# Graph attention prologue: where value stores are issued, when later weights are turned, and in which order attention takes its memory

## The chip, the cores and the metric

The kernel runs on one core of one Trainium2 chip. Its time is the device time in microseconds (us) of one launch; of several runs the median is given. A core has five engines that work side by side, each through its own list of instructions in order: TensorE (PE: matrix products and transposes into PSUM), VectorE (DVE), ScalarE (ACT), GpSimd (POOL) and SyncE (SP), which only issues DMAs. ACT and POOL can issue DMAs too; what an engine issues stands in its own list, between its other work. An engine that waits holds back all that stands behind in its list.

## The reference, cut to what matters

`x` has 3327 rows (N) of 128 features (D), `adj` is 3327 x 3327. There are four layers, each followed by a layer norm over the features:

```
# layer 0, H = 8; Wq, Wk, Wv: 1024 x 128
q = (x @ Wq.T).reshape(128, 3327, 8)      # the flat buffer read anew: d, n, h
k = (x @ Wk.T).reshape(128, 3327, 8)
v = (x @ Wv.T).reshape(128, 3327, 8)
a = einsum('dnh,dmh->dnm', q, k) * 128 ** -0.5 + adj + adj
out = einsum('dnm,dmh->dnh', softmax(a), v).reshape(3327, 1024)
x = layernorm(x + out @ Wo.T)
# layers 1 to 3: products of adj or adj.T with x and small weights
x = layernorm(x + a_norm @ (x @ W1.T + b1))
x = layernorm(x + (adj/deg) @ x @ W_in + (adj.T/deg_T) @ x @ W_out)
x = layernorm(x + x @ W_self.T + (adj @ x) @ W_neigh.T + b3)
```

The attention has 128 "heads" d, each with 3327 queries and keys of length 8. Its exponentials, 128 x 3327 x 3327 of them, are the bulk of the work.

## The kernel before, in words

There are three stages.

**Prologue** (lines 248 to 409). The tokens are taken in seven blocks u of 512 (NU = 7, the last is half full). For each block `split` (342) forms the query products, then the key products: up to four tiles of 128 x 1024 in PSUM (`products`, L292), each copied by ACT into a rounded part `hi` (L348), with the remainder `lo` formed by DVE (L349). POOL issues the stores of both to the DRAM images `q_s` and `k_s` (`store_slots`, L286). DVE also takes the block's largest `hi` (L351, `top_q`, `top_k`). `values_projected` (306) forms the values (L311), copied to `vp` by DVE and ACT in turn (`copy`, L144 and L146). `values_turned` (315) then brings the values into the layout that attention reads: some 42 small products a block (L330) into PSUM, copied to `vo` (again L144/L146). Whenever sixteen d are turned, four stores of `vo` to the image `v_img` go out, issued from ACT (L339), 1.66 MB together. In blocks 1 to 4 a row block of `adj` is loaded (`ar`, L370) and its row maxima taken by DVE (L371); in block 4 (`store_tops`, L219) they are split into `rhi` and `rlo`, and POOL issues their stores to `lead_s` (L228), element by element. `vo` and `ar` share two buffers (tag "wide"), `hi` and `lo` have two each, so a new one waits until the store or the use of the one before the last is over.

After the loop the weights of the later layers are loaded, transposed on PE and stored to DRAM (lines 376 to 388: `w1T`, `w3T`, and the eight pieces of `woT`; the stores are issued from POOL). Then `flag` is formed: a bound on the scores from `top_q` and `top_k`, taken over all partitions with `partition_all_reduce` on POOL (L394), then three small operations of DVE. It decides after attention whether a slow, safe version is to be run. Last, constants are stored to `klead_s` and `k_s` (402 to 409).

The order of the prologue isn't the order of the text: a scheduler places each engine's instructions by their dependences. So some of the text's last parts run early.

**Attention** (412 to 706). 7 column blocks of 476 queries x 4 key ranges make 28 blocks b; in each, 32 groups g of four d. For each d PE forms scores (L625) on top of the transposed `adj` (`e_in`, L618), ACT takes the exponentials (L633; a part runs on DVE), and PE weighs the values with them (L651). The order is written out by hand for PE, ACT, POOL and DVE (`manual_schedule`). Loads are issued from SP: `load_edges` (432, L442, one part per 128 queries, four in all, the last with 92 rows), `load_heads` (460) with queries `qt` (L479), keys `kt` (L486), constant rows of the keys (L492) and, for the first group of a column block, rows from `lead_s` into `qt` (L501), and `load_values` (518, L522). `copy_queries` (506) completes `qt` on DVE (L510 to L512). Memory for these tiles comes from pools that are entered one after the other: accumulators `acc` and value pads (`accp`), `kq` (`kt`, `qt`, `vs`), `ed` (`e_in`), `ex` (exponentials), `pe2`. They take over the memory that the prologue's pools leave, in that order, so a tile's first write waits for the last use of what lay there. `prepare` (557) is called ahead of each d.

DMAs issued from SP and ACT share eight completion semaphores in turn; a DMA that gets one waits until the DMA eight places earlier has landed.

**Later layers** (from line 1000): products with `adj` and its transpose.

Of the kernel before, what the change touches and what calls it, by code (L numbers as in the profile page):

```python
# [10 lines left out]
F32 = mybir.dt.float32  # L11
# [3 lines left out]
ALU = mybir.AluOpType  # L15
AX = mybir.AxisListType
# [3 lines left out]
P = 128  # L20
GROUP = 4
# [15 lines left out]
QK_SAFE = 20.0  # L37
# [13 lines left out]
def kernel(ctx: ExitStack, tc: tile.TileContext, x, adj, wq, wk, wv, wo,  # L51
# [14 lines left out]
    nc = tc.nc  # L66
# [67 lines left out]
    rowsum = const.tile([P, T], F32, name="rowsum")  # L134
    colsum = const.tile([P, T], F32, name="colsum")
    flag = const.tile([P, 1], I32, name="flag")


    rsum = const.tile([P, NU, 4], F32, name="rsum")
# [108 lines left out]
    with tc.tile_pool(name="pw", bufs=1) as pw, tc.tile_pool(name="pa", bufs=2) as pa, \  # L248
# [43 lines left out]
                nc.tensor.matmul(pp[:, c:c + 512], lhsT=xT[:, u, r, :], rhs=w[:, c:c + 512], start=True, stop=True)  # L292
            return pp.rearrange("p (h j) -> p h j", h=H)

        top_q = pw.tile([P, NU], F32, name="top_q")
        top_k = pw.tile([P, NU], F32, name="top_k")

# [15 lines left out]
        def values_turned(d):  # L315

            g, i = d // 16, d % 16
            if i == 0:
                vo[g] = pa.tile([P, 4, T, 32], F32, tag="wide", name="vo")
            ps = pps.tile([P, 2, H, T], F32, tag="ps", bufs=3, name="vtr")  # L320
            for k in range(2):
                q, r = (d + k) * N // D, (d + k) * N % D
                for wrap in range(2 if r else 1):
                    at = q + wrap
                    while at < q + wrap + T:
                        u = at // SUPER
                        n = min(q + wrap + T, (u + 1) * SUPER) - at
                        s = at - q - wrap
                        first = (0 if wrap else P) + r
                        nc.tensor.matmul(ps[:, k, :, s:s + n], lhsT=turn[:, first:first + P],  # L330
                                         rhs=vp[u][:, :, at - u * SUPER:at - u * SUPER + n],
                                         start=(k == 0 and wrap == 0 and s == 0), stop=True,
                                         skip_group_check=True)
                        at += n
            copy(d // 2, vo[g][:, i // 4, :, i % 4 * H:(i % 4 + 2) * H].rearrange("p s (k h) -> p k h s", k=2), ps)
            if i == 14:
                for k0, nt in KBS:
                    w = nt * 32
                    nc.scalar.dma_start(out=flat_ap(v_img, k0 * HD + g * 4 * w, [[T * HD, P], [w, 4], [1, w]]),  # L339
                                        in_=vo[g][:, :, k0:k0 + nt, :].rearrange("p g s c -> p g (s c)"))  # L340

        def split(u, w, s, top, f):
# [11 lines left out]
            store_slots(nc.gpsimd, s, H, u, lo.bitcast(F32))  # L354


        tops = pw.tile([P, 4], F32, name="tops")

        d = 0
        for u in range(NU):  # L360
            split(u, wqT, q_s, top_q, SCALE / 2)
            split(u, wkT, k_s, top_k, 1.0)
            values_projected(u)
            last = u * SUPER + spread(u)[1] * P
            while d < D and (d + 1) * N // D + T < last:
                values_turned(d)
                d += 2
            if 1 <= u <= 4:
                ar = pa.tile([P, NP], F32, tag="wide", name="ar")
                load_rows(nc.sync, ar[:, 0:N], adj, u - 1)  # L370
                nc.vector.tensor_reduce(tops[:, u - 1:u], ar[:, 0:N], AX.X, ALU.max)  # L371
            if u == 4:
                store_tops(pw, 0, tops, P)
        assert d == D

        w1T = load_transposed(pw, ppw, w1, "w1T")
        nc.gpsimd.dma_start(out=w1T_s, in_=w1T.rearrange("p a b -> p (a b)"))
        w3T = load_transposed(pw, ppw, w3, "w3T")
        nc.gpsimd.dma_start(out=w3T_s, in_=w3T.rearrange("p a b -> p (a b)"))

        wo_raw = pw.tile([P, HD], F32, tag="w_raw", name="wo_raw")
        nc.sync.dma_start(out=wo_raw, in_=wo)
        woT = pw.tile([P, HD], F32, name="woT")
        for h in range(H):
            ps = ppw.tile([P, P], F32, tag="w_ps", name="w_ps")
            nc.tensor.transpose(ps, wo_raw.rearrange("p (j h) -> p h j", h=H)[:, h, :], ident)
            copy(h, woT[:, h * D:(h + 1) * D], ps)
        nc.gpsimd.dma_start(out=woT_s, in_=woT)

        top = pw.tile([P, 2], F32, name="top")  # L390
        nc.vector.tensor_reduce(top[:, 0:1], top_q, AX.X, ALU.max)
        nc.vector.tensor_reduce(top[:, 1:2], top_k, AX.X, ALU.max)
        topall = pw.tile([P, 2], F32, name="topall")
        nc.gpsimd.partition_all_reduce(topall, top, P, bass.bass_isa.ReduceOp.max)  # L394
        bound = pw.tile([P, 1], F32, name="bound")
        nc.vector.tensor_tensor(bound, topall[:, 0:1], topall[:, 1:2], ALU.mult)

        nc.vector.tensor_scalar(bound, bound, QK_SAFE / H / 1.001, None, ALU.is_gt)
        nc.vector.tensor_copy(flag, bound)


        zero = pw.tile([4 * H, 512], F32, name="zero")
        nc.vector.memset(zero, 0.0)
        one = pw.tile([1, 512], F32, name="one")
        nc.vector.memset(one, 1.0)
        nc.sync.dma_start(out=klead_s, in_=zero)
        for row in (0, 1):
            nc.sync.dma_start(out=klead_s[row:row + 1, :], in_=one)
        nc.sync.dma_start(out=k_s[:, SLOTS:RS], in_=zero[0:2 * H, :])


    def attention():
        with tc.tile_pool(name="acc", bufs=1) as accp, tc.tile_pool(name="kq", bufs=3) as kq, \
                tc.tile_pool(name="ed", bufs=1) as ed, tc.tile_pool(name="ex", bufs=1) as ex, \
                tc.tile_pool(name="pe2", bufs=1) as pe, \
                tc.tile_pool(name="psc", bufs=1, space=PSUM) as psc:
            NG = (NHG + PACK - 1) // PACK
# [42 lines left out]
            def load_heads(b, g):  # L460

                c0, kb = blocks[b]
                k0, nt = KBS[kb]
                ns = [(nt + 1) // 2, nt // 2]
                kt = kq.tile([P, GROUP, 4 * P], F32R, name="kt")
                qt = kq.tile([P, GROUP, CW], F32R, name="qt")  # L470
                qf = qt.bitcast(F32)
                kf = kt.bitcast(F32)

                d = g * GROUP
                if kb:
                    for half in range(2):
                        nc.sync.dma_start(out=qf[64 * half:64 * half + 64].rearrange("p a c -> p (a c)"), in_=qimg[g])
                for row, a, n in ((0, 0, 2 * H), (1, H, H), (1 + 2 * H, 0, H)) if kb == 0 else ():
                    nc.sync.dma_start(out=qf[row:row + 2 * n - 1:2],  # L479
                                      in_=flat_ap(q_s, a * RS + c0 + d * N, [[RS, n], [N, GROUP], [1, CW]]))  # L480
                for back in range(2):
                    j = 1 if back and g == 0 else 0
                    for rg in range(2):
                        for u in range(2):
                            row = 64 * rg + 32 * back + u
                            nc.sync.dma_start(  # L486
                                out=kf[row:row + 31:2, j:, 0:ns[rg] * P],
                                in_=flat_ap(k_s, (d + j - back) * N + (k0 + (ns[0] if rg else 0)) * P,
                                            [[RS, 16], [N, GROUP - j], [1, ns[rg] * P]]))
                if g == 0:  # L490
                    for rg in range(2):
                        nc.sync.dma_start(out=kf[64 * rg + 32:64 * rg + 64, 0, 0:ns[rg] * P],  # L492
                                          in_=klead_s[:, 0:ns[rg] * P])
                if g == 0 and kb == 0:
                    nc.vector.memset(qf[32:64, 0], 0.0)
                    u = c0 // SUPER
                    cut = min(CW, (u + 1) * SUPER - c0)
                    for uu, a, n in ((u, 0, cut), (u + 1, cut, CW - cut)):
                        for row, part in ((0, 0), (16, 1), (1, 1), (17, 0)):
                            if n:  # L500
                                nc.sync.dma_start(  # L501
                                    out=qf[32 + row:33 + row, 0, a:a + n],
                                    in_=flat_ap(lead_s[uu], part * SUPER + c0 + a - uu * SUPER, [[SUPER, 1], [1, n]]))
                return kt, qt
# [169 lines left out]
                        in_=acc[32 * j:32 * j + nb * A1, f, :])  # L674


            queue, place = [], 0
            with tc.manual_schedule(engines={mybir.EngineType.PE, mybir.EngineType.Activation,
                                             mybir.EngineType.Pool, mybir.EngineType.DVE}):
                for j in range(len(subs)):  # L680
# [5 lines left out]
                values[groups[0]] = load_values(*groups[0])  # L686
                for b, d in steps:
                    prepare(b, d)
                    for si in range(len(SETS[KBS[blocks[b][1]][1]])):
                        vector_work(b)  # L690
                        exponents(b, d, si)
# [573 lines left out]
```

## Time and profile before

| What | us |
|---|---|
| median of 3 runs | 10760.09 |
| lowest and highest | 10756.05, 10763.08 |
| span of the profiled execution | 10769.0 |
| of it PE busy | 10578.8 |
| ACT busy | 9583.6 |
| DVE busy | 7959.0 |
| POOL busy | 1555.0 |
| first exponential of attention starts (L633) | 337.22 |
| first load of the later layers issued (L1013) | 10007.39 |

The profile is of one execution, whose only time is its span. Its times are counted from the start of that span. "Busy" leaves out the issuing of DMAs; the timeline shows it in rows with a "q" behind the engine (ACTq, SPq, POOLq). A row's bracket gives how long the engine stood idle before it and what ended that. A product on PE is listed as MATMUL, its weights' load as LDWEIGHTS (PEld), which runs beside the product before it.

### The profile page before, as it was taken

To read this page: it belongs to the slowest core of one execution; us is meant where nothing else is said; L and a number is where in the kernel's file an instruction comes from. 1 tells how busy PE (TensorE), PEld (TensorE's weight loads), DVE (VectorE), ACT (ScalarE), POOL (GpSimd) and SP (SyncE) were. 2 spreads that over 40 slices of the span, in tenths; PEclk is the share of its full clock that TensorE was granted. 3 is DMA by queue.
4 is the path that set the end of the run, shared out by engine and by line. 5 is a ranking of instruction groups with operands and counts; after the bars stand their busy time and mean duration, and the time that the engine had idled before them with its cause. 6 is when DMAs were issued, how large, how long until landed. Compare 5 with 4: busy or idle time off the path is not lost. (4 is left out here: it accounts for less than half of the span.)

```text
span 10769.0 us, 200811 instructions
## 1 busy us (share of the span) xinstructions
PE 10578.8 (98%) x76941; PEld 4110.9 (38%) x76941; DVE 7959.0 (74%) x8554; ACT 9583.6 (89%) x10447; POOL 1555.0 (14%) x2742
## 2 busy tenths in 40 slices
PE   8899999999999999999999999999999999999999
PEld 5333333333333333333333333333333333333779
DVE  6677788877788778887788777878777777777412
ACT  3799999999999999999999999999999999999400
POOL 0111122111221111211122111121111100001200
PEclk9999999999999999999999999999999999999999
DMA  7678897788976889768888688886888867888676
GB/s 250 187 183 189 205 212 183 178 194 199 211 191 168 199 203 209 192 170 193 198 209 200 156 192 189 198 195 171 194 194 201 195 162 178 181 188 197 220 281 246
DMA packets 1013555, 2116.45 MB, mean 197 GB/s; under 512 B 206760, under 2 KB 730730, under 8 KB 998772
## 3 DMA queue, kind: packets, MB, share of 16 engines
q1 hardware_dynamic: 915358, 1972.12, 75.8%
q0 software_dynamic: 79616, 116.88, 3.7%
q8 instruction: 623, 10.21, 0.4%
q10 hardware_dynamic: 17620, 14.49, 0.4%
q14 instruction: 338, 2.76, 0.1%
HBM read 1863.03 MB, written 239.54 MB: 195 GB/s over the span
## 5 line engine op out<-in xcount | busy, mean ns | idle before, releaser
L633 ACT ACTIVATE e<-sc 128x952 f32<-128x952 f32 (+1 forms) x9968 | 9361.2, 1085 | 322.8 <-PE sc L625 295.0
L651 PE MATMUL o<-e,v_pad 128*32 128x476 f32 (+1 forms) x46592 | 5650.9, 573 | 43.2 <-DVE acc L664 18.6
L625 PE MATMUL sc<-qt,kt 64*128 64x476 f32 x23296 | 4494.8, 440 | 55.8 <-ACT e L633 33.9
L625 PEld LDWEIGHTS sc<-qt,kt 64*128 64x128 f32 x23296 | 2184.3, 184 | 4439.7 <-ACT e L633 3736.3
L595 DVE SCALAR_TENSOR_TENSOR e<-e,ey 128x952 f32<-128x952 f32 x2352 | 2706.5, 1151 | 77.4
L589 DVE TENSOR_SCALAR ey<-sc 128x952 int32<-128x952 f32 x784 | 901.2, 1149 | 1426.5 <-PE sc L625 1389.1
L651 PEld LDWEIGHTS o<-e,v_pad 128*32 128x32 f32 (+1 forms) x46592 | 1035.8, 108 | 1914.8 <-issue 1893.1
L526 POOL COPY v_pad<-vs 128x192 f32<-128x192 f32 (+1 forms) x896 | 439.0, 516 | 8029.8 <-DMA vs<-v_img 6501.4
L595 DVE SCALAR_TENSOR_TENSOR e<-ey 128x952 f32<-128x952 f32 x784 | 903.0, 1152 | 27.2
L595 DVE SCALAR_TENSOR_TENSOR e<-e,et 128x952 f32<-128x952 f32 x784 | 901.5, 1150 | 22.2
L237 POOL DMA_DIRECT2D adjT_s<-at x1352 | 760.4, 570 | 141.5 <-DMA adjT_s<-at 99.2
L590 DVE TENSOR_SCALAR et<-ey 128x952 int32<-128x952 int32 x784 | 519.5, 663 | 26.9
L592 DVE TENSOR_SCALAR ey<-ey 128x952 int32<-128x952 int32 x784 | 518.9, 662 | 27.1
L1101 PE MATMUL bank<-y,eT 128*128 128x128 f32 (+1 forms) x4056 | 473.9, 276 | 0.4 <-DVE h L1223 0.4
L1101 PEld LDWEIGHTS bank<-y,eT 128*128 128x128 f32 (+1 forms) x4056 | 465.3, 192 | 5.7 <-DVE h L1223 0.6
L664 DVE TENSOR_TENSOR acc<-o,acc 128x476 f32<-128x476 f32 x231 | 150.3, 651 | 284.5 <-PE o L651 284.0
L510 DVE TENSOR_SCALAR qt<-qt 32x1428 fp32r<-32x1428 f32 x224 | 201.8, 901 | 93.3 <-DMA qt<-q_s 64.2
L1061 ACT ACTIVATE rstd<-mv,eps 128x1 f32<-128x1 f32 x104 | 30.4, 293 | 265.2 <-DVE mv L1059 265.2
L512 DVE CAST qt<-qt 64x1904 fp32r<-64x1904 f32 x224 | 259.9, 1160 | 7.6
L671 POOL DMA_DIRECT2D o_s<-acc x308 | 200.4, 655 | 35.3 <-DVE acc L664 21.2
L1204 PE MATMUL bank<-a,y 128*128 128x512 f32 (+2 forms) x364 | 145.5, 562 | 0.0
L348 ACT ACTIVATE hi<-pp 128x1024 fp32r<-128x1024 f32 x52 | 52.7, 1024 | 95.4 <-PE pp L292 78.2
(151 smaller groups left out, 2286.6 us busy)
## 6 DMA issues: line engine op xcount, KB each, us to landing
qt<-qimg SPq DMA_DIRECT2D x1344, 476.0 KB
kt<-k_s SPq DMA_DIRECT2D x5320, 96.0 KB
kt<-k_s SPq DMA_DIRECT2D x1764, 128.0 KB
eT<-adjT_s SPq DMA_DIRECT2D x78, 1664.0 KB
qimg<-qt SPq DMA_DIRECT2D x224, 476.0 KB
vs<-v_img SPq DMA_DIRECT2D x224, 224.0 KB
adjT_s<-at POOLq DMA_DIRECT2D x1352, 32.0 KB, 5.0
vs<-v_img SPq DMA_DIRECT2D x224, 192.0 KB
```

Source lines behind the costliest of these rows:

```text
L237: nc.gpsimd.dma_start(out=flat_ap(adjT_s, (t * P + 32 * q) * NP + c * PIECE, [[NP, 32], [P, ns], [1, P]]), in_=at[32 * i:32 * i + 32].rear ...
L510: return [(0.9, None, lambda: nc.vector.tensor_scalar(qt[32:64, 1:], qf[0:32, 0:GROUP - 1], -1.0, None, ALU.mult)), (0.4, None, lambda: nc ...
L512: (1.2, None, lambda: nc.vector.tensor_copy(qt[64:128], qf[0:64]))]
L526: nc.gpsimd.tensor_copy(vp[:, 32:32 + nt * GROUP * 32].rearrange("p (x c) -> p x c", c=32)[:, :, 0:H], vs.rearrange("p (x c) -> p x c", c=H))
L589: nc.vector.tensor_scalar(yi, x, -58 * math.log(2.0), 2 ** 24 / math.log(2.0), ALU.max, ALU.mult)
L590: vec.append((0.7, of, lambda: nc.vector.tensor_scalar(ti, yi, UPPER, EXPONENT, ALU.bitwise_and, ALU.bitwise_xor)))
L592: vec.append((0.7, of, lambda: nc.vector.tensor_scalar(yi, yi, LOWER, QUARTER, ALU.bitwise_and, ALU.bitwise_or)))
L595: vec.append((1.2, of, lambda i=i, a=a: nc.vector.scalar_tensor_tensor(e, e if i else y, a, t if i == len(POLY) - 1 else y, ALU.add, ALU.m ...
L625: nc.tensor.matmul(s[:, i, 0:CW], lhsT=kt[64 * rg:64 * rg + 64, k, pos * P:(pos + 1) * P], rhs=qt[64 * rg:64 * rg + 64, k, :], start=False ...
L633: nc.scalar.activation(e[:, 0:n, :], s[:, 0:n, 0:CW], AF.Exp, scale=2.0)
L651: nc.tensor.matmul(o[32 * j:32 * j + 32, 0:CW], lhsT=values[b, g][:m, c:c + 32], rhs=es[b, g * GROUP + j, r][:m, :], start=(r == 0 and u = ...
L1101: nc.tensor.matmul(ps[:n, 0:D], lhsT=e[:m, s, :n], rhs=y[:m, s, col:col + D], start=(s == 0), stop=(s == T - 1))
```

## The change

The value stores (`v_img`) are issued from SP and no longer from ACT. The later weights are loaded, turned and stored in the loop, behind the values of blocks 2, 3 and 4, and their stores are issued from SP. The constants' stores stand ahead of the loop. `flag` is formed in attention: its reductions are placed at d = 16 of the first block, the rest at d = 32. Attention enters its pools in the order `ed`, `kq`, `acc`, `ex`, `pe2`. The keys of the very first group (b = 0, g = 0) are loaded from ACT's queue.

```diff
@@ ahead of the prologue
+    top_q = const.tile([P, NU], F32, name="top_q")
+    top_k = const.tile([P, NU], F32, name="top_k")
+
+    def set_flag():
+        top = const.tile([P, 2], F32, name="top")
+        nc.vector.tensor_reduce(top[:, 0:1], top_q, AX.X, ALU.max)
+        nc.vector.tensor_reduce(top[:, 1:2], top_k, AX.X, ALU.max)
+        topall = const.tile([P, 2], F32, name="topall")
+        nc.gpsimd.partition_all_reduce(topall, top, P, bass.bass_isa.ReduceOp.max)
+        yield
+        bound = const.tile([P, 1], F32, name="bound")
+        nc.vector.tensor_tensor(bound, topall[:, 0:1], topall[:, 1:2], ALU.mult)
+        nc.vector.tensor_scalar(bound, bound, QK_SAFE / H / 1.001, None, ALU.is_gt)
+        nc.vector.tensor_copy(flag, bound)
+        yield
@@ values_turned
-                    nc.scalar.dma_start(out=flat_ap(v_img, k0 * HD + g * 4 * w, [[T * HD, P], [w, 4], [1, w]]),
+                    nc.sync.dma_start(out=flat_ap(v_img, k0 * HD + g * 4 * w, [[T * HD, P], [w, 4], [1, w]]),
@@ ahead of the loop over blocks
+        def later_weights(i):
+            if i < 2:
+                name, w, dram = (("w1T", w1, w1T_s), ("w3T", w3, w3T_s))[i]
+                wT = load_transposed(pw, ppw, w, name)
+                nc.sync.dma_start(out=dram, in_=wT.rearrange("p a b -> p (a b)"))
+                return
+            wo_raw = pw.tile([P, HD], F32, tag="w_raw", name="wo_raw")
+            nc.sync.dma_start(out=wo_raw, in_=wo)
+            woT = pw.tile([P, HD], F32, name="woT")
+            for h in range(H):
+                ps = ppw.tile([P, P], F32, tag="w_ps", name="w_ps")
+                nc.tensor.transpose(ps, wo_raw.rearrange("p (j h) -> p h j", h=H)[:, h, :], ident)
+                copy(h, woT[:, h * D:(h + 1) * D], ps)
+            nc.sync.dma_start(out=woT_s, in_=woT)
+
+        zero = pw.tile([4 * H, 512], F32, name="zero")
...
+        nc.sync.dma_start(out=k_s[:, SLOTS:RS], in_=zero[0:2 * H, :])
@@ in the loop
             values_projected(u)
+            if 2 <= u <= 4:
+                later_weights(u - 2)
@@ behind the loop: the same weights (stored from gpsimd), flag and constants
-        w1T = load_transposed(pw, ppw, w1, "w1T")
-        nc.gpsimd.dma_start(out=w1T_s, in_=w1T.rearrange("p a b -> p (a b)"))
...
-        nc.sync.dma_start(out=k_s[:, SLOTS:RS], in_=zero[0:2 * H, :])
@@ attention
-        with tc.tile_pool(name="acc", bufs=1) as accp, tc.tile_pool(name="kq", bufs=3) as kq, \
-                tc.tile_pool(name="ed", bufs=1) as ed, tc.tile_pool(name="ex", bufs=1) as ex, \
+        with tc.tile_pool(name="ed", bufs=1) as ed, tc.tile_pool(name="kq", bufs=3) as kq, \
+                tc.tile_pool(name="acc", bufs=1) as accp, tc.tile_pool(name="ex", bufs=1) as ex, \
@@ load_heads: both kinds of key loads
+                keys = nc.sync if b or g else nc.scalar
-                            nc.sync.dma_start(
+                            keys.dma_start(
                                 out=kf[row:row + 31:2, j:, 0:ns[rg] * P],
-                        nc.sync.dma_start(out=kf[64 * rg + 32:64 * rg + 64, 0, 0:ns[rg] * P],
+                        keys.dma_start(out=kf[64 * rg + 32:64 * rg + 64, 0, 0:ns[rg] * P],
@@ the loop of attention
+            flagged = set_flag()
                     prepare(b, d)
+                    if b == 0 and d in (4 * GROUP, 8 * GROUP):
+                        next(flagged)
```

More of the change, by code (lines that the diff above doesn't have):

```diff
@@ L293, in products @@
             return pp.rearrange("p (h j) -> p h j", h=H)
-        top_q = pw.tile([P, NU], F32, name="top_q")
-        top_k = pw.tile([P, NU], F32, name="top_k")
         turn = pw.tile([P, 3 * P], F32, name="turn")
@@ L354, in split @@
             store_slots(nc.gpsimd, s, H, u, lo.bitcast(F32))
-        tops = pw.tile([P, 4], F32, name="tops")
+        def later_weights(i):
[12 more added lines that the diff above has]
+            nc.sync.dma_start(out=woT_s, in_=woT)
+        tops = pw.tile([P, 4], F32, name="tops")
+        zero = pw.tile([4 * H, 512], F32, name="zero")
+        nc.vector.memset(zero, 0.0)
+        one = pw.tile([1, 512], F32, name="one")
+        nc.vector.memset(one, 1.0)
+        nc.sync.dma_start(out=klead_s, in_=zero)
+        for row in (0, 1):
+            nc.sync.dma_start(out=klead_s[row:row + 1, :], in_=one)
+        nc.sync.dma_start(out=k_s[:, SLOTS:RS], in_=zero[0:2 * H, :])
         d = 0
@@ L374 @@
         assert d == D
-        w1T = load_transposed(pw, ppw, w1, "w1T")
-        nc.gpsimd.dma_start(out=w1T_s, in_=w1T.rearrange("p a b -> p (a b)"))
[L378 to L408, printed above, removed]
-        nc.sync.dma_start(out=k_s[:, SLOTS:RS], in_=zero[0:2 * H, :])
     def attention():
-        with tc.tile_pool(name="acc", bufs=1) as accp, tc.tile_pool(name="kq", bufs=3) as kq, \
-                tc.tile_pool(name="ed", bufs=1) as ed, tc.tile_pool(name="ex", bufs=1) as ex, \
+        with tc.tile_pool(name="ed", bufs=1) as ed, tc.tile_pool(name="kq", bufs=3) as kq, \
+                tc.tile_pool(name="acc", bufs=1) as accp, tc.tile_pool(name="ex", bufs=1) as ex, \
                 tc.tile_pool(name="pe2", bufs=1) as pe, \
@@ L674, in store @@
                         in_=acc[32 * j:32 * j + nb * A1, f, :])
-            queue, place = [], 0
+            queue, place, flagged = [], 0, set_flag()
             with tc.manual_schedule(engines={mybir.EngineType.PE, mybir.EngineType.Activation,
```

## The prediction

> **What bounds the kernel now.** I began with the page's slices: TensorE and ScalarE are full from the second slice on, and only the first slice (269 us) has room.
>
> ```profile
> PE   8899999999999999999999999999999999999999
> ACT  3799999999999999999999999999999999999400
> ```
>
> The change touches only the prologue (0 to 337 us, when the first exponential starts) and, in attention, five small instructions of DVE and two of POOL. Comparing the two programs' instruction lists engine by engine, all instructions after the 490th on PE, the 148th on ACT, the 247th on DVE, the 67th on POOL and the 71st on SP are the same, in the same order. So the forecast is: how much earlier does the first exponential start? Next, the prologue in stretches of 20 us (columns: length, busy PE, PEld, DVE, ACT, POOL, granted clock, DMA share, GB/s):
>
> ```profile
> 160.00:180.00 20.00, 19.78 (x84) 14.78 (x83) 16.31 (x13) 6.35 (x7) 2.34 (x3) 0.96 0.84 305
> 200.00:220.00 20.00, 19.38 (x60) 11.48 (x61) 17.10 (x12) 5.95 (x7) 2.66 (x3) 0.85 0.61 228
> 220.00:240.00 20.00, 15.58 (x60) 12.86 (x59) 3.79 (x6) 4.32 (x6) 0.00 (x0) 0.83 0.78 266
> 280.00:300.00 20.00, 8.49 (x17) 4.30 (x17) 9.37 (x7) 5.33 (x9) 7.01 (x11) 0.74 1.02 371
> 300.00:320.00 20.00, 10.05 (x45) 9.29 (x45) 2.88 (x8) 2.98 (x5) 1.59 (x3) 0.79 0.75 227
> 320.00:340.00 20.00, 7.85 (x28) 5.13 (x29) 5.72 (x10) 1.80 (x2) 3.12 (x7) 0.50 0.56 173
> ```
>
> TensorE is nearly full until 280 us; the holes lie at 220 to 240 and above all after 280. The timeline of ScalarE says why in the first two places: its queue issues the value stores, and an issue can last long.
>
> ```profile
> 217.05 9.52 ACTq L339 DMA_DIRECT2D v_img<-vo  x4
> 272.40 13.78 ACTq L339 DMA_DIRECT2D v_img<-vo  x4
> 286.28 1.94 ACT L348 ACTIVATE hi<-pp 128x1024 fp32r<-128x1024 f32 x2 [14.01 <-issue]
> ```
>
> TensorE's waits from 95 to 337 us (total, times, longest) show what reaches it: 9.3 us of L311 and 4.4 us of L330 are these two issues.
>
> ```profile
> PE sc L618 <- DMA e_in<-in_adj_dram: 14.9, 4, 9.9
> PE pp L292 <- DVE lo L349: 10.9, 4, 3.9
> PE pv L311 <- ACT vp L144: 10.5, 3, 9.3
> PE vtr L330 <- ACT vo L144: 5.9, 2, 4.4
> ```
>
> The third hole is the junction to attention: the last turned copy ends at 310.6, the first exponential starts at 337.22, 26.6 us later.
>
> ```profile
> 317.70 1.65 SPq L442 DMA_DIRECT2D e_in<-in_adj_dram  x4
> 321.01 0.37 POOL L394 PARTITION_ALL_REDUCE topall<-top  x1 [6.08 <-DMA e_in<-in_adj_dram]
> 322.09 2.17 SPq L479 DMA_DIRECT2D qt<-q_s  x3
> 324.31 6.70 SPq L486 DMA_DIRECT2D kt<-k_s  x8
> 337.22 1.36 ACT L633 ACTIVATE e<-sc 128x1428 f32<-128x1428 f32 x1 [23.20 <-DMA qt<-q_s]
> ```
>
> **What the Trainium skill says.** "DMA: Bandwidth & Descriptors", section Issuing engines are not separate DMA queues: a store moved to another engine's queue runs on the same 16 DMA engines, and only the issue time is saved. The trace gives that time: eight groups of four stores held ScalarE 3.10, 4.41, 4.62, 6.59, 9.52, 3.07, 13.78 and 3.07, in sum 48.2 us. The same page, Specifications: below 512 B a transfer is a read-modify-write. The trace agrees strongly: the two lead stores (L228, elements of 4 B, 2 KB each) took 11.2 and 20.0 us to land, and the core's DMA fell to 20 GB/s in 260 to 265 and again in 275 to 280. "TensorE: Matmul & The Clock Gate", Part 1: an idle array falls to half clock and needs about 3.4 us of work to recover. Here too: after the 9.3 us hole the clock was 0.50, and eight k products took 6.09 us against 3.60 at 261. "GPSIMD Engine Reference", 1.1: some operations need a library loaded at run time; the 6.08 us idle before L394 fits that.
>
> **Part by part.** *Stores on SyncE.* ScalarE is rid of 48.2 us of issuing. TensorE felt 1.53 (at 182.9) + 4.42 (227.7) + 9.31 (288.5) = 15.3 of it. What is late next decides how much stays.
> - 1.53: nothing. The next wait (3.45 at 199.9) is for DVE, whose row maxima (L371, 3.62 us) wait for `ar`, which shares buffers with `vo` and is loaded after the value stores landed. These start when the copies are ready, on either queue: same time.
> - 4.42: kept at first. But six of the eight `wo` transposes now lie in that stretch with one PSUM buffer between them; four waits of some 0.6 (L386 waited 0.94 and 0.39 before) plus 0.27 each cost about 3. The new order also puts block 5's turning behind all its k products, which wait for DVE (reduction 4.41, then 3.62): in before, the two were interleaved. I take the start of block 6's q products as unchanged, 271 us.
> - 9.31: ScalarE takes block 6's q tiles at once, not at 286. Then late is `lo` of block 6's k: its buffer is free when block 5's `k_s` lo store has landed. In before that store (267.5, 23.7 to landing) landed at 291.2, just ahead of its use at 294.3. In after both lead stores come behind q lo instead of around it, and q lo is finished sooner, since the maxima stand behind it on DVE: leads at some 253 instead of 255.8 and 260.1, two holes of about 7 us to 268, then 4 MB at the 390 GB/s of 280 to 285, 10.8 us, with the value stores beside it: 279 to 291, and I take 283.
>
> From that `lo` to the last turned copy before: 294.3 to 310.6, 16.3. Now three value copies of DVE and not one stand behind it, +0.9: 17.2. So the last copy ends at 283 + 17.2 = 300.2.
>
> *Weights.* One w1 and two w3 transposes already ran amid the prologue, as did five of the eight of `wo`; only three stood at the end, after the last turning matmul. Their stores leave POOL (0.56, 0.57, 0.62) for SP: nothing. Nor do the constants of `klead_s` cost anything: in both built programs they are among SP's first six DMAs.
>
> *Flag.* The first `qt` load waited for it (SP: 2.6 us at L479). It costs attention two reductions and three small operations, 5 x 0.15 = 0.8 us of DVE (81% busy), and 6.4 us of POOL (14% busy). What hides it: a `v_pad` copy is made a group ahead (eleven exponentials of 1.085 us, about 12). Uncovered it would cost at most 6.4, once.
>
> *Pools and second queue.* `e_in` no longer waits for the last stores to land; the first goes out at the last turning matmul, the others behind the four stores (issue 3.1). Through one queue go 1.66 MB of stores and 1.67 MB of `e_in`, at 300 GB/s 11 us; the fourth `e_in` landed 10.5 after its group's issue before, so I put it at +12 from the last copy. Stores landed at +7 before; then `qt` (SP) and `kt` (ACT) start together. But a DMA waits for the one eight places earlier: `kt` 7 and 8 and both `klead` wait for lead loads, and those for the fourth `e_in`. Hence +12, lead 2, four issues 2.4, landing 2, and 2.1 from first matmul to exponential (335.15 to 337.22): 20.5 instead of 26.6. Bounds 17.5 and 24. ScalarE's ten issues come before its first exponential, so nothing waits behind them.
>
> Sum: first exponential at 300.2 + 20.5 = 320.7, against 337.2: 16.5 us less. In the profiled execution 10769.0 becomes 10752.5; its span is 8.9 above the median of the runs, so from the median: 10760.1 - 16.5 = **10743.6**.
>
> **Rivals.** A measurement of this kernel can tell about 0.2% from no change, 21.5 us. (a) *More*: store landed by 279, turning at full clock (9.2 becomes 7.7), junction 17.5, and the gaps of 0.99, 1.50 and 2.31 behind the first exponentials close with the earlier loads: 25 + 4.8 = 30 less, 10730. For it speaks that everything in attention follows the loads; against it that TensorE will again be cold after waiting for the store. (b) *The k store takes the stall's place whole*: landed at 291 as now, junction 24: 291.2 + 17.2 + 24 = 332.4, 4.8 less, 10755. The DMA share of 1.02 in 280 to 300 speaks for it. (c) *Slower*: SyncE's one queue. The value stores wait there for their copies and hold each of the four `ar` loads behind their issue; DVE waits for `ar` already (10.9 us in four waits), so delays of 4.41 + 4.62 + 6.59 + 9.52 = 25.1 would pass through `lo` to TensorE, the gain on block 6 would be eaten by the late `e_in`, and 10760 + 25 = 10785. It decides from about 5.4 us per load. Against it: SP waited 143.7 us at L88 for these same stores to land, so `ar` was behind them anyway. (d) *The change doesn't do what it says*: excluded for the order, which the built program shows.
>
> **Chances.** Forecast 57% (10736 to 10753), (a) 22%, (b) 15%, (c) 6%. Of the forecast's case about 10 points lie beyond 21.5 us. Faster by over 0.2%: 0.22 + 0.10 = 0.32; slower 0.06; within 0.62. The range goes from (a) to (b) with 3 us of scatter (the three runs spread 7): 10729 to 10758.
>
> **What would show it.** No `v_img` issue on ScalarE, and no PE wait over 2 us on ACT; `lo` at 280 to 286 waiting for nothing but the store; last copy near 300; first exponential near 321, after the last `klead`; slices 3 to 40 unchanged. Wrong if PE waits for `lo` grow behind `ar` (c), if the k store lands near 291 (b), or if slices of attention differ.

## The result and the profile after

The changed kernel takes 10741.69 us (median of 20 runs, 10738.76 to 10745.57), the kernel before 10761.24 beside it (20 runs): 19.6 us less, ratio 0.9982, interval 0.9976 to 0.9988, so 13 to 26 us. Forecast were 16.5 less. The interval excludes no change at all; the step is still just under the 21.5 us (0.2%) that the forecast took for what can be told from no change.

The two profiled spans, 10769.0 and 10737.5, differ by 31.5, more than the medians. Where that lies can be counted. The first exponential starts at 317.66 instead of 337.22: 19.6 earlier. From there to the end of the last exponential it is 9648.5 instead of 9660.9, 12.3 less, though the instructions are the same in the same order. In the runs below this stretch takes 9641.7 to 9659.4, and it goes more with the group in which a run was measured than with its edit: 9641.7 to 9646.9 in e1 to e4, 9653.0 to 9659.4 in e5 to e8, 9647.7 to 9654.7 in e9 to e12 (each group on another chip; the kernel before beside them had medians of 10756.4, 10766.4 and 10767.3). One reservation: the kernel before, e5 and e7 start attention last and have the three longest stretches, so that a small share of the 12.3 isn't excluded. It is mostly scatter, and the first exponential is what to compare; it agrees with the medians.

The page's slices of PE and ACT after: only ACT's second slice moves, from 7 to 8.

```profile
PE   8899999999999999999999999999999999999999
ACT  3899999999999999999999999999999999999400
```

The prologue after in stretches of 20 us (columns as in the prediction):

```profile
220.00:240.00 20.00, 18.51 (x66) 11.51 (x65) 9.23 (x9) 7.90 (x10) 1.77 (x2) 1.00 0.93 311
240.00:260.00 20.00, 15.74 (x46) 8.30 (x45) 16.23 (x12) 5.51 (x7) 3.30 (x4) 0.83 0.75 267
...
280.00:300.00 20.00, 11.01 (x50) 9.85 (x49) 5.25 (x7) 3.35 (x5) 3.22 (x6) 0.86 0.86 260
300.00:320.00 20.00, 6.45 (x24) 4.36 (x24) 5.25 (x7) 1.36 (x1) 2.75 (x6) 0.50 0.68 186
320.00:340.00 20.00, 17.33 (x88) 7.57 (x90) 6.44 (x8) 16.59 (x17) 0.69 (x2) 0.71 0.70 189
```

The hole at 220 to 240 is nearly closed (PE 18.5, was 15.6), and what stood in 320 to 340 stands a stretch earlier. A new dip is at 240 to 260 (PE 15.7, was 18.7): a wait of 3.59 for `lo`, at 248.77. PE's waits after, from 95 to 345 us (total, times, longest):

```profile
PE pp L308 <- DVE lo L363: 17.1, 6, 5.5
PE sc L625 <- DMA e_in<-in_adj_dram: 15.7, 4, 6.0
PE sc L632 <- DMA kt<-k_s: 4.3, 1, 4.3
PE pv L325 <- ACT vp L160: 2.3, 4, 0.7
```

Of the waits for ACT, 10.5 for `vp` and 5.9 for `vo`, 2.3 are left; `lo` took 6.2 back (17.1 for 10.9), as one of the waits behind `ar` grew from 3.45 to 5.49. Rows of the timeline after around the last blocks:

```profile
249.09 0.76 POOL L244 DMA_DIRECT2D lead_s<-rhi  x1 [9.27 <-DVE rhi L239]
250.28 0.75 POOL L244 DMA_DIRECT2D lead_s<-rlo  x1 [0.43 <-DVE rlo L241]
256.35 0.90 POOL L302 DMA_DIRECT2D k_s<-hi  x1 [5.31 <-ACT vp L160]
257.30 0.89 POOL L302 DMA_DIRECT2D k_s<-lo  x1
267.57 3.59 SPq L353 DMA_DIRECT2D v_img<-vo  x4
271.90 1.02 ACT L362 ACTIVATE hi<-pp 128x1024 fp32r<-128x1024 f32 x1 [1.42 <-PE pp L308]
277.95 2.35 DVE L363 SCALAR_TENSOR_TENSOR lo<-pp,hi 128x1024 fp32r<-128x1024 f32 x2
```

ACT takes block 6's first query tile at 271.90 and not at 286.28. The last `lo` (277.95) has no bracket: DVE goes from work to work and waits for no store. Behind the leads the DMA engines have one hole of 5 us (columns as in the prediction):

```profile
253.00:258.00 5.00, 5.00 (x21) 3.12 (x20) 3.45 (x3) 2.12 (x3) 1.59 (x2) 0.98 0.05 17
```

Then the junction, from the last turned copy to the first exponential:

```profile
293.21 0.35 SPq L448 DMA_DIRECT2D e_in<-in_adj_dram  x1
293.22 0.85 ACT L160 COPY vo<-vtr 128x416 f32<-128x416 f32 x1 [2.00 <-PE vtr L344]
294.10 3.18 SPq L353 DMA_DIRECT2D v_img<-vo  x4
297.33 2.98 SPq L448 DMA_DIRECT2D e_in<-in_adj_dram  x3
301.81 2.20 SPq L486 DMA_DIRECT2D qt<-q_s  x3
301.90 11.15 ACTq L493 DMA_DIRECT2D kt<-k_s  x8
310.16 2.00 PE L625 MATMUL sc<-ident,e_in 92*128 92x92 f32 x9 [5.14 <-DMA e_in<-in_adj_dram]
313.10 1.26 ACTq L499 DMA_DIRECT2D kt<-klead_s  x2
316.49 1.13 PE L632 MATMUL sc<-qt,kt 64*128 64x476 f32 x3 [4.34 <-DMA kt<-k_s]
317.66 1.36 ACT L640 ACTIVATE e<-sc 128x1428 f32<-128x1428 f32 x1 [23.59 <-DMA kt<-k_s]
```

The last copy ends at 294.1, the fourth part of `e_in` lands at 310.1 (PE's wait for it ends there), the keys at 316.5. The junction is 23.6 (before: 26.6).

### The profile page after: what moved, and what is told of

It reads as the page before. It is cut to its first block, busy times and chain, and to the rows that moved or that the text cites. A ratio compares the mean times of both kernels' runs of the same rounds, so it can differ in the third digit from the quotient of the medians.

```text
span 10737.5 us, 200822 instructions
## 1 busy us (share of the span) xinstructions
PE 10565.1 (98%) x76941; PEld 4105.8 (38%) x76941; DVE 7960.2 (74%) x8554; ACT 9584.8 (89%) x10447; POOL 1554.7 (14%) x2739
## 5 line engine op out<-in xcount | busy, mean ns | idle before, releaser
L658 PE MATMUL o<-e,v_pad 128*32 128x476 f32 (+1 forms) x46592 | 5647.1, 573 | 39.4 <-DVE acc L671 18.5
L602 DVE SCALAR_TENSOR_TENSOR e<-ey 128x952 f32<-128x952 f32 x784 | 903.4, 1152 | 27.2
L597 DVE TENSOR_SCALAR et<-ey 128x952 int32<-128x952 int32 x784 | 518.3, 661 | 26.9
```

Of the source, the lines that this page charges most:

```text
L597: vec.append((0.7, of, lambda: nc.vector.tensor_scalar(ti, yi, UPPER, EXPONENT, ALU.bitwise_and, ALU.bitwise_xor)))
L602: vec.append((1.2, of, lambda i=i, a=a: nc.vector.scalar_tensor_tensor(e, e if i else y, a, t if i == len(POLY) - 1 else y, ALU.add, ALU.m ...
L658: nc.tensor.matmul(o[32 * j:32 * j + 32, 0:CW], lhsT=values[b, g][:m, c:c + 32], rhs=es[b, g * GROUP + j, r][:m, :], start=(r == 0 and u = ...
```

## The experiments

Theory: the gain is the 16.5 us by which the last copy is earlier, from the value stores' leaving ACT's queue, and 3.0 in the junction. The rival gives the junction the main part. Each run has one trace. All twelve runs in one table (us; "junction" is first exponential less end of the last copy; the last columns compare with the kernel before run beside it):

| Run | last copy ends | junction | first exponential | median less before | interval of the ratio |
|---|---|---|---|---|---|
| before | 310.6 | 26.6 | 337.2 | | |
| after | 294.1 | 23.6 | 317.7 | -19.6 | 0.9976 to 0.9988 |
| e1 before, stores on SP | 294.2 | 26.5 | 320.7 | -10.7 | 0.9983 to 0.9999 |
| e2 after, stores on ACT | 299.4 | 26.9 | 326.3 | -9.9 | 0.9985 to 0.9998 |
| e3 after, old pools | 294.6 | 26.2 | 320.8 | -12.1 | 0.9981 to 0.9997 |
| e4 after, keys on SP | 293.8 | 24.1 | 317.9 | -20.2 | 0.9975 to 0.9989 |
| e5 before, weights in loop | 304.2 | 30.5 | 334.8 | -3.9 | 0.9988 to 1.0005 |
| e6 after, weights last | 293.4 | 27.0 | 320.4 | -20.9 | 0.9972 to 0.9988 |
| e7 before, leads late | 306.8 | 26.8 | 333.5 | -4.3 | 0.9988 to 1.0005 |
| e8 after, flag in prologue | 296.0 | 24.0 | 320.1 | -20.7 | 0.9973 to 0.9988 |
| e9 after, fourth part first | 294.3 | 27.2 | 321.5 | -19.4 | 0.9973 to 0.9989 |
| e10 after, fourth part split | 298.2 | 21.9 | 320.1 | -22.2 | 0.9962 to 0.9985 |
| e11 after, both | 296.7 | 21.2 | 317.9 | -25.7 | 0.9963 to 0.9984 |
| e12 after, six lead stores | 303.9 | 24.9 | 328.8 | -15.8 | 0.9978 to 0.9991 |

The runs after, e3, e4, e8, e9, e10 and e11 have the same order up to the last copy, and it ends at 293.8 to 298.2. So 4 us of a single trace's last copy are scatter; the junction, counted from it, leaves that out. The medians' intervals are 13 to 25 us wide: they support the large steps and decide none of the small ones.

**Whose gain it is: e1 and e2.**

```diff
-                    nc.scalar.dma_start(out=flat_ap(v_img, ...
+                    nc.sync.dma_start(out=flat_ap(v_img, ...      # e1: in before; e2: the reverse, in after
```

> The kernel before with one edit: the value stores are issued from SyncE. Theory (the queue): most of the 19.6 us comes from ScalarE being rid of these issues, and from the order that follows (both lead stores together ahead of block 5's key stores). Then the last turned copy ends at 293 to 297 instead of 310.6, the junction stays at about 26 us as in the kernel before, the first exponential starts at 319 to 323, and the time is 14 to 18 us below the kernel before. Rival (the junction): the stores only move a wait, and the gain comes from the pools and the second queue. Then the last copy comes at 304 or later and the time is less than 7 us below the kernel before.

Measured: last copy 294.2, junction 26.5, first exponential 320.7, 16.5 before that of the kernel before.

```profile
293.34 0.85 ACT L144 COPY vo<-vtr 128x416 f32<-128x416 f32 x1 [2.00 <-PE vtr L330]
320.69 1.36 ACT L633 ACTIVATE e<-sc 128x1428 f32<-128x1428 f32 x1 [23.20 <-DMA qt<-q_s]
```

The theory holds in the trace. The median is 10.7 less (1 to 18), short of the 14 to 18 that I expected; it agrees with the trace but can't exclude the rival's 7. This one edit also brings the order of the changed kernel: both lead stores stand together ahead of block 5's keys.

> The changed kernel with the value stores back on ScalarE, all else kept. Theory (the queue): the last turned copy comes at 308 to 312 again, the junction keeps its 23 to 24 us, so the first exponential starts at 331 to 336: only 2 to 5 us below the kernel before, some 15 above the changed kernel. Rival (the junction): the first exponential starts before 326, more than 10 us below the kernel before.

Measured: 326.3, between the two. Taking the stores back costs 8.6, not 15: 5.3 up to the last copy and 3.3 in the junction, where `qt` and `kt` are loaded only from 314.2 and 314.4 on (301.8 and 301.9 in the changed kernel). So my expected last copy, 308 to 312, was wrong. What else of the change works when ACT is held again? Two runs ask.

**The order beside the stores: e5 and e7.**

```diff
# e5, in before: later_weights as in the change
+            if 2 <= u <= 4:
+                later_weights(u - 2)
# e7, in before
-            if u == 4:
+            if u == NU - 1:
                 store_tops(pw, 0, tops, P)
```

> The kernel before with one edit: the later weights are turned in the loop and stored from SyncE; the value stores stay on ScalarE. The forecast said: nothing (within 1 us), the last turned copy near 310. Theory from the run with the stores back on ScalarE (last copy 299.4 although ScalarE was held as in the kernel before): the pieces of wo amid the last block's keys put VectorE's copy of the values behind its 2.28 us reduction, so the last copy ends at 298 to 301 here, the junction stays at 26 to 28, the first exponential starts at 325 to 329, and the time is 8 to 12 us below the kernel before.

Measured: last copy 304.2, later than the 298 to 301 that I expected, and a junction of 30.5, so that only 2.5 arrive. From the end of ACT's long issue to the last copy it is 17.8 (286.4 to 304.2) and in e2 18.6; in the kernel before it is 24.4, in e7, below, 24.8: moving the weights takes 6.6 off this stretch. That it was the pieces of `wo` among the last block's products is argued from their place in the timeline. The junction gives it back: `e_in` goes out at 315.05, 10.8 after the last copy, where the kernel before took 7.1.

> The kernel before with one edit: the two lead stores are made in the last block, which puts both of them together behind block 5's query stores, as in the changed kernel, and no longer around the second of these. The stores of the values stay on ScalarE. Theory: the DMA holes of the two leads fall together, block 5's key stores land at 280 or before instead of 291.2, the 13.78 us value issue on ScalarE shrinks to 6 to 9, and the last turned copy ends at 302 to 306. Rival: ScalarE's issue is as long as before because the stores' own bytes fill it, and the last copy stays at 308 to 311.

Measured: the same four value stores hold ACT for 9.49 instead of 13.78, and block 5's `lo` keys (issued 267.61, the kernel before 267.52) land after 19.6 instead of 23.7. First e7's timeline, then its list of DMA issues (last column: us to landing), then its two DMA holes:

```profile
272.49 9.49 ACTq L339 DMA_DIRECT2D v_img<-vo  x4
282.09 1.94 ACT L348 ACTIVATE hi<-pp 128x1024 fp32r<-128x1024 f32 x2 [9.74 <-issue]
```

```profile
k_s<-lo POOLq DMA_DIRECT2D x1, 2048.0 KB, 19.6
```

```profile
263.00:268.00 5.00, 5.00 (x23) 3.92 (x22) 3.90 (x6) 2.83 (x3) 2.79 (x4) 1.00 0.07 1
270.00:275.00 5.00, 4.90 (x22) 3.57 (x21) 3.98 (x4) 0.86 (x1) 0.00 (x0) 1.00 0.42 20
```

My sizes were too large (last copy 306.8, not 302 to 306, and its 3.8 us are no more than the scatter above), but the hold and the landing bear out the kind: the issue is as long as the transfers ahead are stuck. It ends 5.0 before the `lo` keys land in the kernel before (286.2, 291.2), 5.2 in e7 (282.0, 287.2), 4.9 in e5 (286.4, 291.3), 4.4 in e2 (280.8, 285.1). So, as I read these runs, the stores' gain of 16.5 is an overlap: ACT held by an issue, the issue held by the transfers that the leads' holes delay, and `wo` behind it. With the issue on SP, where nothing waits behind it, all go at once, and the weights' move has nothing left to gain ahead of the last copy (e1 and e6 end it where the changed kernel does). Why e2's issue is 11.5 and e5's 15.3 stays open.

**Does the key store still bound block 6? e12.**

```diff
+                for more in lead_x if n == P else []:
+                    nc.gpsimd.dma_start(out=flat_ap(more, row * SUPER, [[1, n], [n, 4]]), in_=sb.bitcast(F32))
```

> The changed kernel with each lead store made three times, the added ones to scratch that nobody reads: six stores of 2 KB ahead of block 5's key stores instead of two. The forecast's step was that lo of block 6's keys waits for block 5's key store behind the leads. In the changed kernel that store has landed at 270.2 and lo ran at 277.95, 7.7 us of room. Theory (the step is right in kind and its size was off): with the leads' two holes of 5 us more each, or up to 9 each, the store lands at 280 to 289, lo follows it, and the last copy, 294.1 before, ends 2 to 12 us later (store's landing + 16 to 17). Rival: TensorE and its own queue set the last copy, and it stays within 1 us of 294.1 although the store lands after 280.

The keys are issued at 262.98 (257.30 in the changed kernel) and land after 24.1, at 287.1. DVE in e12's timeline:

```profile
287.18 2.36 DVE L366 SCALAR_TENSOR_TENSOR lo<-pp,hi 128x1024 fp32r<-128x1024 f32 x2 [6.34 <-DMA k_s<-lo]
```

Now `lo` waits 6.34 for the store, and the last copy ends 16.7 later, at 303.9. So the chain of the forecast exists, with 16.7 where it had 17.2. The changed kernel runs inside it, with 7.7 to spare: its keys had landed at 270.2, and `lo` ran at 277.95.

**The junction: e3, e4, e6, e8.**

```diff
# e3: pools again acc, kq, ed
# e4
-                keys = nc.sync if b or g else nc.scalar
+                keys = nc.sync
# e6
+        for i in range(3):
+            later_weights(i)          # behind the loop
# e8: set_flag() run through behind the loop
```

> The changed kernel with attention's pools in the order of the kernel before (acc, kq, ed). The first part of e_in then waits again until the last value stores have landed (about +7 us after the last copy). If the pools are what shortened the junction (26.6 to 23.6), it is 26 to 28 here and the first exponential starts at 320 to 322, 2 to 4 us later than in the changed kernel. If the second queue did it, it stays near 318. If the loads first in memory are the main part of the whole gain (rival), the first exponential starts after 325.

Measured: junction 26.2, first exponential 320.8. Without the new order of the pools most of the 3 us are lost.

> The changed kernel with the first group's keys on SyncE as all others. In the changed kernel the chain runs over the landing of the fourth part of e_in (310.1), the constant key rows behind it and their landing (316.4), so the eight key issues of some 5 us on SyncE, done between 304 and 310, would be hidden: the first exponential within 2 us of 317.7, the time the same. If instead the second queue is what shortened the junction, the first exponential comes 3 to 6 us later.

Measured: 317.9, as expected; the eight key issues (304.3 to 311.6) are hidden.

> The changed kernel with the later weights behind the loop again, stores on SyncE kept. If the weights' move and the stores' move take away the same wait (theory: they overlap), the last turned copy ends at 293 to 295 as in the changed kernel, and the first exponential starts at 317 to 321 (the weights' last store now stands on SyncE ahead of e_in). If they are worth 11 us each on their own (rival), the last copy ends after 300.

Measured: last copy 293.4, first exponential 320.4: the two moves overlap ahead of the last copy, and the weights cost in the junction, 3.4.

> The changed kernel with flag formed in the prologue again. Forecast: the 6.1 us of GpSimd before the reduction over partitions and the small operations lie beside the last turning products and the landing of e_in, whose end (310) is later than the flag (before 300): first exponential within 1 us of 317.7, time the same as the changed kernel. Rival: SyncE's first query load waits for flag, and the first exponential comes 3 to 6 us later.

Measured: 320.1, more than my 1 us; but the last copy, ahead of the edit, was 2.0 later, and the junction is 24.0.

e3 and e6 lose the 3 us in the same way. In e3's timeline, then e6's, all four parts of `e_in` go out only when the last stores have landed:

```profile
293.69 0.87 ACT L160 COPY vo<-vtr 128x416 f32<-128x416 f32 x1 [2.00 <-PE vtr L344]
...
301.42 2.01 SPq L448 DMA_DIRECT2D e_in<-in_adj_dram  x4
...
314.47 2.00 PE L625 MATMUL sc<-ident,e_in 92*128 92x92 f32 x9 [4.19 <-DMA e_in<-in_adj_dram]
```

```profile
296.57 1.24 SPq L384 DMA_DIRECT2D woT_s<-woT  x1
...
301.52 2.07 SPq L448 DMA_DIRECT2D e_in<-in_adj_dram  x4
...
312.86 2.00 PE L625 MATMUL sc<-ident,e_in 92*128 92x92 f32 x9 [3.40 <-DMA e_in<-in_adj_dram]
```

So the pools' order and the weights' move are both needed for the same 3 us: one without the other leaves `e_in` behind a store (junction 26.2 and 27.0). SP stood waiting 3.3 for the value stores in e3 and 3.6 for `woT`'s store in e6. The second queue is worth 0.5 (e4) and flag's move 0.4 (e8); a single trace each can't tell either from nothing.

**What holds the fourth part: e9, e10, e11.** In the trace after, the DMA engines are busy at only 0.21 to 0.30 in each of the last microseconds (308 to 311) before and at the fourth part's landing:

```profile
308.00:309.00 1.00, 0.00 (x0) 0.00 (x0) 0.00 (x0) 0.00 (x0) 0.00 (x0) 0.50 0.30 107
309.00:310.00 1.00, 0.00 (x0) 0.00 (x0) 0.00 (x0) 0.00 (x0) 0.00 (x0) 0.50 0.27 93
310.00:311.00 1.00, 0.84 (x4) 0.85 (x5) 0.00 (x0) 0.00 (x0) 0.00 (x0) 0.50 0.21 73
```

```diff
# e9 (and e11)
-                for j in range(len(subs)):
+                for j in (0, 3, 1, 2):
                     load_edges(0, j)
# e10 (and e11)
+                for a, m in ([(0, 80), (80, n - 80)] if b == 0 and n < P else [(0, n)]):
```

> The changed kernel with the four parts of the first e_in loaded in the order 0, 3, 1, 2. Theory: the junction's chain runs over the landing of the fourth part (issued 299.5, landed 310.1, the lead loads and the constant key rows behind it). Issued second, at 297.3, it lands at 306 to 308; the first exponential starts 2 to 4 us earlier than in the changed kernel, at 313.5 to 316. Rival: the keys' landing from ScalarE's queue is as late on its own, and the first exponential stays at 317 to 318. A time 2 to 4 us lower is below what the medians can tell; the trace decides.

> The changed kernel with the first column block's fourth e_in part (92 rows) loaded as 80 and 12 rows, the order of the parts as in the changed kernel. From 307 to 310 the DMA engines were busy at only 0.21 to 0.30 with that part alone, as if a quarter of them carried it. Theory: split, it is spread over more of them and lands at 305 to 307 instead of 310.1; the first exponential starts at 313.5 to 316. Rival: the tail is the keys and queries that share the engines; the landing and the first exponential stay within 1 us.

> The changed kernel with both edits: order 0, 3, 1, 2, and the fourth part as 80 and 12 rows. Theory: the fourth part is landed by 304 to 306, the chain then runs over the third part and the keys: first exponential 311.5 to 315, the lowest of all runs, the time 3 to 6 us below the changed kernel. Rival (the keys decide): within 1 us of the better of the two single edits or of 317.7.

None of the three reached the first exponential that I expected: 321.5 (313.5 to 316 expected), 320.1 (313.5 to 316) and 317.9 (311.5 to 315). In e10 and e11 the last copy, ahead of the edit, came 4.1 and 2.6 later than in the changed kernel, so the junctions, 21.9 and 21.2, are what to compare. e11's 317.9 by itself is what the rival forecast. e9 contradicts its theory: with the fourth part put second, the parts behind it become late. e9's timeline, then e11's:

```profile
311.49 0.47 PE L625 MATMUL sc<-ident,e_in 128*128 128x128 f32 x1 [13.91 <-DMA e_in<-in_adj_dram]
313.64 2.21 PE L625 MATMUL sc<-ident,e_in 128*128 128x128 f32 x10 [1.68 <-DMA e_in<-in_adj_dram]
```

```profile
306.89 0.47 PE L626 MATMUL sc<-ident,e_in 128*128 128x128 f32 x1 [6.76 <-DMA e_in<-in_adj_dram]
308.98 2.22 PE L626 MATMUL sc<-ident,e_in 128*128 128x128 f32 x10 [1.62 <-DMA e_in<-in_adj_dram]
```

All parts are there 19.3 us after the last copy in e9, 16.1 in the changed kernel, 13.3 in e10 and 12.3 in e11. The Trainium skill, "DMA: Bandwidth & Descriptors", section Why a DMA increments its semaphore by 16 and not by 1, has a rule that fits: a DMA runs on the largest number of engines, at most 16, that divides its outermost size, here 92 rows: four. Four of 16 are 0.25; the trace shows 0.21 to 0.30. The steps of the completion semaphores, which the traces also keep, show the count itself: the fourth part lands in four single steps (309.30 to 310.11 in the changed kernel), each full part in 16; in e10 and e11 the piece of 80 rows lands in 16 and that of 12 rows in twelve. Here are 305 to 310 as a whole (changed kernel, then e11; the last two columns are DMA share and GB/s):

```profile
305.00:310.00 5.00, 0.02 (x1) 0.00 (x0) 0.00 (x0) 0.00 (x0) 0.00 (x0) 0.50 0.68 144
```

```profile
305.00:310.00 5.00, 1.49 (x6) 1.21 (x7) 0.08 (x1) 0.00 (x0) 2.26 (x6) 0.50 1.00 289
```

In e11, with 80 and 12 rows, the engines are full (0.92 or more in each microsecond from 301 on) until all parts have landed, at 309. The same steps explain e9: of the 16 of each full part behind the fourth, twelve came by 305.1 and 307.1, the last four only at 310.0 to 311.4 and 311.4 to 313.6, after the fourth part's own four (307.0 to 309.2). So a full part is held by a few engines that still carry the fourth. e11 has the shortest junction, 2.4 below the changed kernel, and beside e10 the lowest ratio, 0.9973, but its interval overlaps that of the changed kernel: shown in the trace, not in the time.

## Why the prediction was right

The total and its main reason were right: 16.5 forecast, 19.6 measured, the last copy earlier because ACT is no longer held (e1: the stores alone bring 16.5). Two terms were off, in opposite directions: 6.1 too little up to the last copy, 3.1 too much in the junction. That the total came within 3.1 is partly luck, since they cancelled in part.

- *ACT's holds.* Right: PE's longest wait for ACT in the prologue is 0.7. That 1.53 and 4.42 would be given back to `lo` was right in kind: its waits grew by 6.2. Six of block 6's eight query products start at 270.8, forecast 271; the other two had run at 255.6.
- *"two holes of about 7 us to 268, then 4 MB ... 10.8 us ... I take 283"*: this step failed. The leads were issued at 249.1 and 250.3, not 253; the DMA engines had older work until 253, and only one hole of 5 us followed (253 to 258, DMA share 0.05), not two of 7. POOL had no store of keys to issue in it before 256.35, so this hole need not be the leads' doing. The keys' last store, issued at 257.3, took 12.9 and had landed at 270.2. So block 6's `lo` was bound by the chain of products, `hi` and reductions and ran at 277.95, below my bounds of 279 to 291: 5 us to the good. e12 shows the mechanism itself, once the store is late enough. Why the leads held up nothing behind 258 stays open: they were issued 7 us ahead of the keys and behind older transfers, in e7 3 us ahead of the keys and with no older work; no run separates the two.
- *17.2 from `lo` to the last copy*: 16.1 (e12: 16.7).
- *Junction 20.5*: 23.6, the term that was too small. Of it, "the fourth `e_in` at +12" was +16.1; what follows took 7.5, I had 8.5. I had shared 3.3 MB over all engines at 300 GB/s; the last part ran on four of them (e10, without that: +13.3).
- *Weights: nothing.* Wrong: without this move the junction is 3.4 longer (e6), since `e_in` waits 3.6 on SP for `woT`'s store to land. I had looked for it on PE and POOL and not asked what `e_in` waits for.
- *Flag and constants: hidden.* Right (e8; the reduction over partitions ran at 376 with 6.1 us of idle POOL ahead, and ACT's waits after the first exponential are 1.12, 1.11 and 2.17, before 0.99, 1.50 and 2.31).
- *Rivals.* (a) needed a junction of 17.5 and closed gaps: neither came. (b) needed the key store at 291: it landed at 270.2. (c) needed late `ar` loads: they were issued at 102.4, 142.2, 185.1 and 235.9, each 2 to 7 earlier than before, and SP's wait ahead of them fell from 143.7 to 20.4. SP does hold 8.69 for the stores at 213.7, as ACT held 9.52; right behind it stands only `woT`'s store.
- *The clock.* The forecast spoke of about 3.4 us of work until the clock recovers. In the kernel before it stayed at 0.50 in all of 288 to 294, with 5.5 us of PE work in it: longer than that.

Sum: -16.5 up to the last copy (10.4 forecast), -3.0 in the junction (6.1 forecast).

## What to carry to other kernels

In these runs an engine that issued stores was held as long as older transfers were stuck (3.07 us at best, 9.5 to 15.3 behind the leads). Put such an issue on a queue whose next instruction has time. Don't take the held time for the gain: ACT was held for 48.2 us in all, PE had waited 15.3 for it, and the stores alone brought 16.5, which the order behind them had a part in. When loads of a new stage take over the memory of the old one, follow every store that still stands ahead of them: here the order of pools and the move of the weights gained 3 us together and nothing one by one. Give a load that ends a chain a row count that spreads over the DMA engines: 80 and 12 rows in place of 92 made the junction 1.7 and 2.4 shorter in the traces (e10, e11), too little for the times to show.

## What the runs showed that I had not expected

- A load of 92 rows landed in four steps and ended at a DMA share of 0.21 to 0.30; cut into 80 and 12, it landed in 16 and twelve. Sent earlier, it made full loads behind it late (311.5 and 313.6 instead of 303.4 and 304.5), each by its last four steps.
- Two stores of 2 KB in elements of 4 B, issued back to back 3 us ahead of the keys, came with two holes (e7: 1 GB/s in 263 to 268, before any key transfer, and 20 in 270 to 275, with the keys issued); the keys landed after 19.6. Issued 7 us ahead of the keys, they came with one of 5 us, in which little else was issued, and the keys landed after 12.9 (the changed kernel). Six such stores held the DMA engines to 10 to 129 GB/s in each 2 us from 260 to 276, and the keys landed after 24.1 (e12).
